# Part of a graph network's gathers loaded row by row through SyncE's queue, with two one-bank PSUM tiles and two input buffers

## The chip, the cores and the metric

The kernel runs on one core of a Trainium2 chip. The metric is the device time of one execution in microseconds (us). Five engines work side by side, each from a queue of its own: TensorE (PE in the profile), VectorE (DVE), ScalarE (ACT), GpSimd (POOL) and SyncE (SP). An engine takes its queue in order: an instruction that waits holds up everything behind it on that engine. SP computes nothing; its queue issues DMA transfers. POOL issues the gathers.

## The reference

Two layers of message passing over one graph of 6250 nodes and 200000 edges, sorted by destination. Every node has 160 float32 features: 64 scalars and 32 vectors of three components. Layer 0 takes 10 inputs per edge for its edge network, layer 1 takes 64; each ends with a residual sum and a layer norm.

```python
def layer(x, src, dst, edge_attr, edge_inputs):        # both layers, cut to what matters
    h = mix(x)                                         # per node, a matrix for scalars, one for vectors
    w = silu(edge_inputs @ W1) @ W2                    # per edge: 192 (layer 0) or 224 (layer 1) weights
    g = h[src]                                         # gather: one row of 160 per edge
    m = products(w, g, edge_attr)                      # per edge: scalar and vector messages
    agg = segment_sum(m, dst, num_segments=6250)       # sum over the edges of a node
    return layernorm(x + node_network(x, agg))
```

The whole computation is float32.

## The kernel before

**Tiles and units.** The edges are cut into 1563 tiles of 128 edges, one edge to a partition; four tiles make a unit, so a layer has 391 units (`windows`, L565). The mixed features `h` of all nodes lie in HBM as `table[0]` (written in a prologue) and `table[1]` (written during layer 0, once a block of nodes is done). Two tiles make a pair; `g`, the gathered rows of a pair, has 8 buffers, thus four units' worth.

**One iteration of the unit loop** (L793 and on), for `u` from -4: the gathers of unit `u + 4` (`gather`, four indirect DMAs, each of 128 rows of 640 bytes, on POOL, L681); the second product of the edge network for unit `u + 2` (`weights`, PE into the PSUM tiles `pw`); the first product for unit `u + 3` (`hidden`, PE into `pair`, then Silu on ACT, L643 and L654); the placement matrices (`places`, DVE, L712) and the messages (`products`, DVE, L699) for unit `u + 2`; and the sum of unit `u` over destination windows (`aggregate`, PE into `pg`). A window that ends is turned and added to the node sums `sm` and `sr` (`turn`, L759 and L761, its place read by a register load on DVE, L756). Between these stand the steps of finished node blocks (`prepare`, `proceed`), which load `nx` (L471 in layer 0, L533 and `no`, L534, in layer 1) through SP.

**Inputs.** The edge network's inputs come in chunks of eight tiles, two units. `inputs` (L603) loads a chunk through SP into one of three buffers, `inputs_of[c % 3]`: two DMAs in layer 0 (L612), four in layer 1 (L620). `hidden` asks for the present chunk and the next. The indices `src` and edge attributes `ea` come for 48 tiles at a time, in two buffers (L589, L590), through SP as well.

**PSUM.** `pair` is one tile of two banks of 512 floats. `hidden` writes its first 256 columns, of both banks in layer 0 and of bank `u % 2` in layer 1; `turn` writes the last 256 columns of bank `g % 2`.

**Order.** A scheduler orders the instructions of each engine from the program's text and its own estimates; the waits for buffers and data are put in by the same framework. PE's products are kept in the program's order (L137 to L145). DMAs of SP take eight semaphores in turn, and one waits until the DMA eight before it has landed.

A check of the destinations (L303) chooses between the path above and a general one; these inputs take the path above.

Of the kernel before, what the change touches and what calls it, by code (L numbers as in the profile page):

```python
# [9 lines left out]
F32 = mybir.dt.float32  # L10
# [17 lines left out]
EC = 8  # L28
BG = 4
ZERO = 8  # L30
ROWS = P * NB + P
EPS = 1e-5
C_S = math.sin(math.pi / 8.0)
# [53 lines left out]
def kernel(ctx: ExitStack, tc: tile.TileContext, a, out):  # L87
# [25 lines left out]
    dram = ctx.enter_context(tc.tile_pool(name="dram", bufs=1, space=bass.MemoryType.DRAM))  # L113


    pair = psum.tile([P, 2, 512], F32, name="pair", bufs=1)

    tail_n, tail_e = N - (NB - 1) * P, E - (NT - 1) * P
    table = [dram.tile([N, D], F32, name=f"table{i}") for i in range(2)]
# [89 lines left out]
    fc1 = [const.tile([P, 100], F32, name="fc1_0"), const.tile([P, P], F32, name="fc1_1")]  # L209
    for t in fc1:  # L210
        nc.gpsimd.memset(t, 0.0)
    for r in (0, 64):
        nc.gpsimd.dma_start(fc1[0][r:r + 10], a["W_fc1"])

    fc2 = [const.tile([100, 192], F32, name="fc2_0"), const.tile([P, 224], F32, name="fc2_1")]
    for c0, at, n in ((64, 0, 64), (0, 64, 64), (128, 128, 64)):
# [32 lines left out]
    def turn_nodes(bs, x):  # L249

        m, n = len(bs), rows_of(bs[0])
        p = psum.tile([P, 512], F32, name="pw", bufs=3)
        for j in range(m):
            transpose(p[:, j * P:j * P + n], x[:n, j, 0:P], ident[:n, :n])
        last = work.tile([P, BG * V], F32, name="xz")
        nc.vector.tensor_copy(last[:n, :m * V].rearrange("p (j d) -> p j d", d=V), x[:n, 0:m, P:D])
        z = pair[:, 0, 0:P]
        transpose(z[:m * V, :n], last[:n, :m * V], ident[:n, :n])
        xt = work.tile([P, BG * P], F32, name="xt", bufs=2)
        zt = work.tile([P, P], F32, name="zt", bufs=2)  # L260
        w = (m - 1) * P + n
        if (bs[0] // BG) % 2:
            nc.scalar.activation(xt[:, :w], p[:, :w], AF.Copy)
        else:
            nc.vector.tensor_copy(xt[:, :w], p[:, :w])
        nc.scalar.activation(zt[:m * V, :n], z[:m * V, :n], AF.Copy)
        return xt, zt

    def send_nodes(bs, xt, zt):
        n = rows_of(bs[0])  # L270
        rows = work.tile([P, BG, D], F32, name="rg", bufs=2)
        qs = []
        for j in range(len(bs)):
            tag, k = (("pg", 2), ("pn", 1), ("pg", 2), (None, 0))[j]
            p = psum.tile([P, 512], F32, name=tag, bufs=k) if tag else pair[:, 1]
# [51 lines left out]
        nc.vector.tensor_reduce(tops[:, 1:2], limits, AX.XY, OP.max)  # L327

    def checked():
        p = pair[:, 0]  # L330
# [66 lines left out]
    for k in range(2):  # L397
        nc.vector.tensor_copy(
            rr0[k * V:k * V + V, :, k * V:k * V + V],
            p[k * V:k * V + V, 192:256].rearrange("p (j d) -> p j d", j=2))  # L400

    nc.sync.dma_start(fc1[1][:64, :64], a["fc_w1"])
    nc.sync.dma_start(fc1[1][64:, 64:], a["fc_w1"])
    for r in (0, 64):
# [157 lines left out]
        return [fetch], [summed]  # L562


    def windows(i, loads, work, inputs_of):  # L565
        nw = (192, 224)[i]


# [34 lines left out]
        def inputs(c):  # L603

            e0 = c * EC * P
            n = min(EC * P, E - e0)
            k, of_e = ((10, a["e10"]), (64, a["e64"]))[i]
            e = inputs_of[c % 3]

            for h in range(2):  # L610
                if i == 0 and n == EC * P:
                    nc.sync.dma_start(  # L612
                        e[h * 64:h * 64 + k].rearrange("p (u m) -> p u m", m=2 * P),
                        of_e[:, e0:e0 + n].rearrange("p (u h m) -> p u h m", h=2, m=2 * P)[:, :, h])
                    continue
                for u in range(0, n, 4 * P):
                    r = u + h * 2 * P
                    m = min(2 * P, n - r)
                    if m > 0:
                        nc.sync.dma_start(e[h * 64:h * 64 + k, u // 2:u // 2 + m],  # L620
                                          of_e[:, e0 + r:e0 + r + m])
            made["e", c] = e

        def hidden(u):

            t0 = 4 * u
            c = t0 // EC
            for k in (c, c + 1):
                if ("e", k) not in made and k * EC < NT:
                    inputs(k)  # L630
            e = made["e", c]
            n = min(4 * P, E - t0 * P)
            h = work.tile([P, 512], F32, name="h", bufs=2)
            at = (t0 % EC) * P // 2
            m = min(n, 2 * P)
            if i == 0:

                halves = [(0, m)] + [(1, n - m)] * (n > m)
                for j, m in halves:
                    k = slice(64 * j, 64 * j + 64)  # L640
                    matmul(pair[:100, j, :m], fc1[0][k], e[k, at:at + m], start=True, stop=True)
                for j, m in halves:
                    nc.scalar.activation(h[:100, 2 * P * j:2 * P * j + m], pair[:100, j, :m], AF.Silu)  # L643
            else:
                p = pair[:, u % 2]
                k = P if n > 2 * P else 64
                if n == 4 * P or n <= 2 * P:
                    parts = ((k, 0, m),)
                else:
                    parts = ((P, 0, n - 2 * P), (64, n - 2 * P, 2 * P))  # L650
                for kk, c0, c1 in parts:
                    matmul(p[:kk, c0:c1], fc1[1][:kk, :kk], e[:kk, at + c0:at + c1],
                           start=True, stop=True)
                    nc.scalar.activation(h[:kk, c0:c1], p[:kk, c0:c1], AF.Silu, scale=0.125)  # L654
            made["h", u] = h

        def weights(ps):
# [5 lines left out]
            for p, j in [(p, j) for p in ps for j in range(2)] if i == 0 else \  # L663
                    [(p, j) for j in range(2) for p in ps]:
                t = 2 * p + j
                if t < NT:
# [5 lines left out]
                        l, r = h[k, j * P:j * P + n], fc2[1][k]  # L672
                    matmul(made["w", p][:n, j, :nw], l, r, start=True, stop=True)

        def gather(p):
            g = work.tile([P, 2, D], F32, name="g", bufs=8)
            for j in range(2):
                t = 2 * p + j
                if t < NT:
                    n = edges_of(t)  # L680
                    nc.gpsimd.indirect_dma_start(  # L681
                        out=g[:n, j, :], out_offset=None, in_=table[i][:, :],
                        in_offset=bass.IndirectOffsetOnAxis(ap=of(t)[0], axis=0))
            made["g", p] = g
# [60 lines left out]

        def turn(g):
            r = made["r", g]
            pt = pair[:, g % 2, 2 * P:]
            if i == 0:
                transpose(pt[:96, :P], r[:, :96], ident)  # L750
                transpose(pt[:64, P:P + W], r[:32, 96:160], ident[:32, :32])
            else:
                transpose(pt[:, :P], r[:, :P], ident)
                matmul(pt[:, P:P + W], rest[g % 3], fold, start=True, stop=True)
            with tc.issue_after(made["last"].ins):
                b = nc.vector.value_load(base[0:1, g:g + 1], min_val=0, max_val=NP - W)  # L756
# [36 lines left out]
        for u in range(-4, units + 1):  # L793
# [3 lines left out]
            if u + 4 < units:  # L797
                for p in pairs_of(u + 4):
                    gather(p)
            if 0 <= u + 2 < units:  # L800
                weights(pairs_of(u + 2))
            if 0 <= u + 3 < units:
# [136 lines left out]
    with tc.If(ok > 0) as cmp:  # L939
        with tc.tile_pool(name="loads", bufs=2) as loads, \  # L940
                tc.tile_pool(name="edges", bufs=2) as work:

            inputs_of = [loads.tile([P, EC * P // 2], F32, name=f"e{k}", bufs=1) for k in range(3)]
            for e in inputs_of:
                nc.vector.memset(e, 0.0)
            for i in range(2):
                windows(i, loads, work, inputs_of)
    with cmp.Else():
        pinned[0] = False
        for i in range(2):  # L950
# [53 lines left out]
```

## Time and profile before

| | us |
|---|---|
| median of 3 runs | 4153.65 (4151.93 to 4154.42) |
| the profiled execution's own time | 4153.7 |
| its span, first to last instruction | 4151.9 |
| busy PE / DVE / POOL / ACT | 3476.9 / 3103.4 / 3018.9 / 1151.1 |
| gathers on POOL (L681) | 3126, 2997.0 busy |

Lines of the profile name a source line (L681 is line 681 of the kernel before), the engine, the operation, and output and input tiles. A group's line ends with its busy time, the mean duration of one in ns, and the idle time of the engine ahead of it, with what ended most of that. "issue" is idle time for which the profile shows no wait. A line of waits has the waiting engine and tile, what released it, the us in total, how often, and the longest. SPq and DVEq are the queues of SP and DVE, where DMA issues, register loads (TENSOR_LOAD), register operations (FUSED_REGOPS) and semaphore instructions are seen; they are not counted as busy. Lines of a source line's instructions give the durations as minimum/median/maximum in ns.

### The profile page before, as it was taken

Reading aid. Unit: us, or ns where it says so; the run is one execution under the profiler, and the core shown is the slowest. Engines: PE = TensorE matmul, PEld = TensorE weight load, DVE = VectorE, ACT = ScalarE, POOL = GpSimd, SP = SyncE. Lnnn points to the kernel's source line nnn. Section 1 sums busy time; section 2 is a strip of 40 time slices with the busy share of each in tenths; the row PEclk is TensorE's granted clock in tenths of the full one; section 3 lists DMA queues with packets and bytes.
Section 4 is the critical chain, followed back from the end, with each engine's and each line's share of the span. In section 5 each row is a group of like instructions: output and inputs, shape, how many; then the busy total and the mean of one; then the engine's idle time right before and its main releaser. Section 6 shows DMA issues by size and latency. Waiting matters only on the chain.

```text
span 4151.9 us, 108120 instructions
## 1 busy us (share of the span) xinstructions
PE 3476.9 (84%) x37265; PEld 2397.6 (58%) x37265; DVE 3103.4 (75%) x13202; ACT 1151.1 (28%) x3915; POOL 3018.9 (73%) x3233
## 2 busy tenths in 40 slices
PE   6888888888999999999977888788787778778887
PEld 4655666566666666666655555455555555555555
DVE  5776666677777777777757777778878888888887
ACT  2111112222223333333321111112223333334444
POOL 3777777777777777776637777777777777777774
PEclk8888889999989999999978888888889999999988
DMA  3222222222233333332223333333333333433332
GB/s 118 72 72 73 76 76 78 79 79 80 79 83 81 83 86 86 85 84 78 76 67 95 95 96 99 98 93 105 100 99 101 105 102 99 108 104 104 104 103 59
DMA packets 305442, 369.59 MB, mean 89 GB/s; under 512 B 87103, under 2 KB 253128, under 8 KB 304888
## 3 DMA queue, kind: packets, MB, share of 16 engines
q0 software_dynamic: 151088, 257.36, 23.6%
q1 hardware_dynamic: 125176, 88.36, 7.5%
q10 hardware_dynamic: 28624, 16.88, 1.3%
q8 instruction: 299, 4.90, 0.5%
q14 instruction: 255, 2.09, 0.2%
HBM read 341.50 MB, written 20.80 MB: 87 GB/s over the span
## 4 chain that ended last, share of the span: by engine, by line
PE 29%; issue 21%; DMA 16%; POOL 15%; DVE 15%; ACT 2%; DVEq 1%; SPq 0%; ACTq 0%; POOLq 0%
DMA g<-table,src 16%; POOL g L681 15%; DVE mid L699 9%; PE pw L138 8%; PE pn L138 7%; PE pg L138 7%; PE pair L138 4%; DVE sel L712 2%; PE pair L143 2%; DVE sm L759 1%; DVEq L756 1%; PE pn L143 1%; ACT L458 1%; DVE sr L761 0%; DVE nx L460 0%
## 5 line engine op out<-in xcount | busy, mean ns | idle before, releaser
L681 POOL DMA_INDIRECT g<-table,src x3126 | 2997.0, 959 | 1088.9 <-issue 722.5
L699 DVE TENSOR_TENSOR mid<-g,pw 128x128 f32<-128x128 f32 (+2 forms) x7820 | 1857.1, 302 | 679.5 <-DMA g<-table,src 463.2
L138 PE MATMUL pw<-fc,h 100*128 100x192 f32 (+1 forms) x6252 | 1188.2, 383 | 133.9 <-DVE mid L699 126.0
L138 PE MATMUL pg<-mid,sel 128*32 128x160 f32 (+1 forms) x25008 | 1170.5, 311 | 0.0
L138 PEld LDWEIGHTS pw<-fc,h 100*128 100x128 f32 (+1 forms) x6252 | 870.2, 203 | 301.3 <-issue 233.6
L138 PEld LDWEIGHTS pg<-mid,sel 128*32 128x32 f32 x25008 | 782.4, 119 | 400.6 <-issue 320.0
L712 DVE SCALAR_TENSOR_TENSOR sel<-iota,off,ea 128x128 f32<-128x128 f32 x3126 | 948.1, 345 | 49.8 <-PE pg L138 35.0
L138 PE MATMUL pair<-e,fc 64*100 64x256 f32 (+1 forms) x2348 | 612.2, 467 | 301.3 <-DVE sr L761 288.1
L138 PEld LDWEIGHTS pair<-e,fc 64*100 64x100 f32 (+1 forms) x2348 | 242.4, 188 | 533.7 <-DVE sr L761 369.9
L643 ACT ACTIVATE h<-pair 100x256 f32<-100x256 f32 x782 | 257.6, 381 | 1018.9 <-PE pair L138 980.3
L654 ACT ACTIVATE h<-pair 128x256 f32<-128x256 f32 x392 | 150.5, 384 | 1021.4 <-PE pair L138 1018.7
L143 PE MATMUL pair<-ident,r 128*96 128x128 f32 (+1 forms) x852 | 227.5, 290 | 104.7 <-DVE sr L761 49.7
L143 PEld LDWEIGHTS pair<-ident,r 128*96 128x96 f32 (+1 forms) x852 | 105.5, 124 | 288.5 <-issue 99.1
L759 DVE TENSOR_TENSOR sm<-pair,sm 96x128 f32 (+1 forms) x568 | 163.2, 287 | 90.8 <-PE pair L143 33.2
L737 ACT ACTIVATE r<-pg 128x96 f32<-128x96 f32 (+1 forms) x568 | 149.9, 264 | 292.6 <-PE pg L138 219.8
L743 ACT ACTIVATE rest<-pg 32x32 f32<-32x32 f32 x1136 | 209.6, 184 | 12.5
L138 PE MATMUL pn<-rm,sm 96*128 96x128 f32 (+4 forms) x980 | 179.5, 339 | 26.7 <-DVE sm L759 25.4
L138 PEld LDWEIGHTS pn<-rm,sm 96*128 96x128 f32 (+3 forms) x980 | 164.9, 222 | 35.6 <-DVE sm L759 29.1
L458 ACT ACT_TABLE_LOAD x97 | 124.5, 1283 | 8.6 <-DVE mv L457 7.0
L138 PE MATMUL pn<-rr,sr 64*128 64x128 f32 (+2 forms) x196 | 62.0, 403 | 53.5 <-DVE sr L761 51.6
L138 PEld LDWEIGHTS pair<-fold,rest 128*128 128x128 f32 x568 | 106.4, 229 | 0.0
L761 DVE TENSOR_TENSOR sr<-pair,sr 64x32 f32 (+1 forms) x568 | 101.6, 179 | 0.8 <-DVE sm L759 0.6
(134 smaller groups left out, 1228.9 us busy)
## 6 DMA issues: line engine op xcount, KB each, us to landing
g<-table,src POOLq DMA_INDIRECT x3126
e<-in_e SPq DMA_DIRECT2D x781, 64.0 KB
e<-in_e SPq DMA_DIRECT2D x390, 20.0 KB
ea<-in_ea_main SPq DMA_DIRECT2D x63, 96.0 KB
xself<-no ACTq DMA_DIRECT2D x48, 96.0 KB
no<-xself SPq DMA_DIRECT2D x48, 96.0 KB
xg<-in_x_main SPq DMA_DIRECT2D x12, 320.0 KB
table<-rg SPq DMA_DIRECT2D x12, 320.0 KB
```

What stands on the lines that cost most here:

```text
L138: r = nc.tensor.matmul(*args, **kw)
L143: r = nc.tensor.transpose(*args)
L458: nc.scalar.activation(mv[:n, 1:2], mv[:n, 1:2], AF.Sqrt, bias=eps[:n])
L643: nc.scalar.activation(h[:100, 2 * P * j:2 * P * j + m], pair[:100, j, :m], AF.Silu)
L654: nc.scalar.activation(h[:kk, c0:c1], p[:kk, c0:c1], AF.Silu, scale=0.125)
L681: nc.gpsimd.indirect_dma_start(out=g[:n, j, :], out_offset=None, in_=table[i][:, :], in_offset=bass.IndirectOffsetOnAxis(ap=of(t)[0], axis=0))
L699: nc.vector.tensor_tensor(parts(mid[:n, :m], V * place, V * step, k), parts(g[:n, :m], c, V, k), parts(q[:n, :m], w, w_step, k), OP.mult)
L712: made["last"] = nc.vector.scalar_tensor_tensor(s[:n, j], iota[:n, None, :].to_broadcast([n, 4, W]), w, e[:, :, None].to_broadcast([n, 4, ...
L737: nc.scalar.activation(r[:, :w], pg[:, :w], AF.Copy)
L743: nc.scalar.activation(rest[g % 3][k, k], pg[k, P:P + V], AF.Copy)
L759: nc.vector.tensor_tensor(sm[:h, :, at], pt[:h, :P].rearrange("p (c w) -> p c w", c=4), sm[:h, :, at], OP.add)
L761: made["last"] = nc.vector.tensor_tensor(sr[:k, at], pt[:k, P:P + W], sr[:k, at], OP.add)
```

## The change

- Four units of each layer, 80, 160, 240 and 320, are no longer gathered by POOL. Their rows, 512 a unit, are loaded one by one through SP, some 1.6 partitions (6.4 rows) in each iteration of the unit loop, into one buffer `gs`. For a partition, SP loads the four sources of its edges from SBUF into registers, and issues four DMAs of one row whose address comes from a register. They are kept in the program's order on SP. The next unit's rows begin in the iteration after the one that multiplies the last unit's rows.
- `row_src` holds the sources of these units, loaded by four DMAs before layer 0.
- `inputs_of` has two buffers in place of three.
- `pair` becomes two tiles of one bank each; nothing else is done with them.
- One of the two loads of `W_fc1` goes from POOL's queue to SP's, further down in the prologue.

```diff
+ROW_UNITS = range(80, (NT + 3) // 4 - 1, 80)
...
-    pair = psum.tile([P, 2, 512], F32, name="pair", bufs=1)
+    pair = [psum.tile([P, 512], F32, name=f"pair{k}", bufs=1) for k in range(2)]
...
-    for r in (0, 64):
-        nc.gpsimd.dma_start(fc1[0][r:r + 10], a["W_fc1"])
+    nc.gpsimd.dma_start(fc1[0][0:10], a["W_fc1"])
...
+    nc.sync.dma_start(fc1[0][64:74], a["W_fc1"])
...
-            e = inputs_of[c % 3]
+            e = inputs_of[c % 2]
...
-                    matmul(pair[:100, j, :m], fc1[0][k], e[k, at:at + m], start=True, stop=True)
+                    matmul(pair[j][:100, :m], fc1[0][k], e[k, at:at + m], start=True, stop=True)
...
-                p = pair[:, u % 2]
+                p = pair[u % 2]
...
+        def in_order(r):
+            tc.keep_in_program_order(r)
+
+        def rows_of_unit(u):
+
+            k = next((k for k, x in enumerate(ROW_UNITS) if x - 4 >= u), None)
+            if k is None:
+                return
+            x = ROW_UNITS[k]
+            begin = (ROW_UNITS[k - 1] - 1) if k else -4
+            if u < begin:
+                return
+            if u == begin:
+                made["rows", x] = work.tile([P, 4, D], F32, name="gs", bufs=1)
+            g, steps = made["rows", x], x - 4 - begin
+            k0, k1 = ((v * P + steps - 1) // steps for v in (u - begin, u - begin + 1))
+            for p in range(k0, min(k1, P)):
+                loads_, v = nc.values_load_multi_w_load_instructions(
+                    row_src[p:p + 1, k, :], engines=[ET.SP], min_val=0, max_val=N - 1,
+                    skip_runtime_bounds_check_because="an edge's source is a node")
+                for r in loads_:
+                    in_order(r)
+                for j in range(4):
+                    in_order(nc.sync.dma_start(g[p:p + 1, j, :], table[i][bass.ds(v[j], 1), :]))
+
         def gather(p):
+            if p // 2 in ROW_UNITS:
+                made["g", p] = made["rows", p // 2][:, 2 * (p % 2):2 * (p % 2) + 2, :]
+                return
...
-            pt = pair[:, g % 2, 2 * P:]
+            pt = pair[g % 2][:, 2 * P:]
...
                 for p in pairs_of(u + 4):
                     gather(p)
+            rows_of_unit(u)
             if 0 <= u + 2 < units:
                 weights(pairs_of(u + 2))
...
-            inputs_of = [loads.tile([P, EC * P // 2], F32, name=f"e{k}", bufs=1) for k in range(3)]
+            inputs_of = [loads.tile([P, EC * P // 2], F32, name=f"e{k}", bufs=1) for k in range(2)]
             for e in inputs_of:
                 nc.vector.memset(e, 0.0)
+            row_src = loads.tile([P, len(ROW_UNITS), 4], I32, name="row_src", bufs=1)
+            for k, u in enumerate(ROW_UNITS):
+                nc.sync.dma_start(row_src[:, k, :], a["src_main"][:, 4 * u:4 * u + 4, 0])
```

More of the change, by code (lines that the diff above doesn't have):

```diff
@@ L256, in turn_nodes @@
         nc.vector.tensor_copy(last[:n, :m * V].rearrange("p (j d) -> p j d", d=V), x[:n, 0:m, P:D])
-        z = pair[:, 0, 0:P]
+        z = pair[0][:, 0:P]
         transpose(z[:m * V, :n], last[:n, :m * V], ident[:n, :n])
@@ L274, in send_nodes @@
             tag, k = (("pg", 2), ("pn", 1), ("pg", 2), (None, 0))[j]
-            p = psum.tile([P, 512], F32, name=tag, bufs=k) if tag else pair[:, 1]
+            p = psum.tile([P, 512], F32, name=tag, bufs=k) if tag else pair[1]
             q = p[:n, :2 * D].rearrange("p (w d) -> p w d", w=2)
@@ L329, in checked @@
     def checked():
-        p = pair[:, 0]
+        p = pair[0]
         transpose(p[:1, :P], over, ident)
@@ L562, in last_nodes, with windows @@
         return [fetch], [summed]
-    def windows(i, loads, work, inputs_of):
+    def windows(i, loads, work, inputs_of, row_src):
         nw = (192, 224)[i]
@@ L640, in hidden @@
                     k = slice(64 * j, 64 * j + 64)
-                    matmul(pair[:100, j, :m], fc1[0][k], e[k, at:at + m], start=True, stop=True)
+                    matmul(pair[j][:100, :m], fc1[0][k], e[k, at:at + m], start=True, stop=True)
                 for j, m in halves:
-                    nc.scalar.activation(h[:100, 2 * P * j:2 * P * j + m], pair[:100, j, :m], AF.Silu)
+                    nc.scalar.activation(h[:100, 2 * P * j:2 * P * j + m], pair[j][:100, :m], AF.Silu)
             else:
-                p = pair[:, u % 2]
+                p = pair[u % 2]
                 k = P if n > 2 * P else 64
@@ L941 @@
                 tc.tile_pool(name="edges", bufs=2) as work:
-            inputs_of = [loads.tile([P, EC * P // 2], F32, name=f"e{k}", bufs=1) for k in range(3)]
+            inputs_of = [loads.tile([P, EC * P // 2], F32, name=f"e{k}", bufs=1) for k in range(2)]
             for e in inputs_of:
                 nc.vector.memset(e, 0.0)
+            row_src = loads.tile([P, len(ROW_UNITS), 4], I32, name="row_src", bufs=1)
+            for k, u in enumerate(ROW_UNITS):
+                nc.sync.dma_start(row_src[:, k, :], a["src_main"][:, 4 * u:4 * u + 4, 0])
             for i in range(2):
-                windows(i, loads, work, inputs_of)
+                windows(i, loads, work, inputs_of, row_src)
     with cmp.Else():
```

## The prediction

> **What bounds the kernel now.** I read the page first. It gives GpSimd (POOL) 73% of the span and TensorE (PE) 84%, so the busy shares don't name the bound. The group of the gathers, L681, does: 1088.9 us of idle time stand before them, and 722.5 us of it waited for nothing.
>
> ```profile
> span 4151.9 us, 108120 instructions
> PE 3476.9 (84%) x37265; PEld 2397.6 (58%) x37265; DVE 3103.4 (75%) x13202; ACT 1151.1 (28%) x3915; POOL 3018.9 (73%) x3233
> ...
> L681 POOL DMA_INDIRECT g<-table,src x3126 | 2997.0, 959 | 1088.9 <-issue 722.5
> ```
>
> Second, the timeline of POOL alone. The gathers stand back to back, 0.95 us each and 0.30 us of issue between them, 1.255 us from start to start.
>
> ```profile
> 1001.21 0.95 POOL L681 DMA_INDIRECT g<-table,src  x1 [0.30 <-issue]
> 1002.47 0.95 POOL L681 DMA_INDIRECT g<-table,src  x1 [0.30 <-issue]
> 1003.72 0.95 POOL L681 DMA_INDIRECT g<-table,src  x1 [0.30 <-issue]
> ```
>
> Third, busy time by stretch (the fifth pair of numbers is POOL's time and count): 317 gathers in 400 us of the first layer and 318 in the second, so a unit of four gathers takes 400/317 x 4 = 5.05 us and 5.03 us. VectorE (DVE) is busy for 268 and 332 of the 400 us. Both layers run at the pace of POOL.
>
> ```profile
> 480.00:880.00 400.00, 339.65 (x3670) 239.65 (x3661) 268.16 (x1066) 85.98 (x268) 303.63 (x317) 0.89 0.29 77
> 3320.00:3720.00 400.00, 311.61 (x3637) 217.72 (x3637) 331.58 (x1517) 140.79 (x512) 303.39 (x318) 0.92 0.38 103
> ```
>
> Fourth, POOL's waits. Only the third column's long ones are true stalls: 52.2 us until the first table stands, 51.2 us between the layers, and some of the 147.9 us for a free `g` buffer.
>
> ```profile
> POOL g L681 <- issue: 722.5, 2370, 0.3
> POOL g L681 <- DVE mid L699: 147.9, 377, 4.1
> POOL g L681 <- DMA g<-table,src: 52.4, 172, 0.3
> POOL g L681 <- DVE rr L398: 52.2, 1, 52.2
> POOL g L681 <- DMA e<-in_e: 51.5, 2, 51.2
> ```
>
> Last, SyncE's queue (SP), on which the change puts its work. It waits for most of the run, because it is ahead: for free input buffers, and for gathers that still use a `src` tile. That is room, and the question is whether it is enough.
>
> ```profile
> SPq L612 <- PE pair L138: 1178.6, 157, 15.2
> SPq L589 <- DMA g<-table,src: 878.7, 160, 25.8
> SPq L620 <- PE pair L138: 712.0, 237, 13.1
> ```
>
> **Removed from POOL.** Four units a layer (80, 160, 240, 320), four gathers each: 32 gathers x 1.255 us = 40 us, 20 us a layer. The later consumers have slack to take it (DVE 67% and 83% busy). So if all else stays hidden, 4153.7 - 40 = 4114 us. 4153.7 us is the profiled execution's own time, 1.8 us over its span and 0.05 us over the median of the runs, 4153.65; sums are made on it.
>
> **Added to SP.** For each of the 128 partitions of such a unit: one load of four registers, four register operations (row number to address), four DMAs of 640 bytes. That is 1024 loads, 4096 register operations and 4096 DMAs, in a queue that holds some 1,500 DMAs now. None of this form is in the trace of before; the nearest rows are these (ns, minimum/median/maximum):
>
> ```profile
> L756 DVEq TENSOR_LOAD <-base x568: 296/303/478, 111.2 to 4139.1; - x190
> L756 DVEq FUSED_REGOPS  x568: 190/190/206, 111.6 to 4139.5; - x190
> L938 SPq TENSOR_LOAD <-flag x1: 476/476/476, 75.8 to 75.8; - x1
> L938 SPq FUSED_REGOPS  x1: 186/186/186, 76.3 to 76.3; - x1
> L471 SPq DMA_DIRECT2D nx<-in_x_main x48: 351/352/461, 77.9 to 2003.6; - x48
> L471 SPq DMA_DIRECT2D nx<-in_x_tail x1: 251/251/251, 2035.7 to 2035.7; - x1
> L612 SPq DMA_DIRECT2D e<-in_e x390: 282/283/1256, 79.4 to 2057.4; - x195
> L620 SPq DMA_DIRECT2D e<-in_e x784: 314/556/1843, 2063.4 to 4091.3; - x196
> ```
>
> Between two instructions of a queue the trace leaves some 0.045 us, 0.08 us after a register load.
> - The register operation: 0.19 us (both rows).
> - The row's DMA: between 0.25 us (the tail of `nx`, the cheapest load of SP) and 0.47 us (the loads of a 64-row tail, L592). I take 0.27 us, near the short ones, since a row is small.
> - The load of four registers: a load of one takes 0.30 us. The Trainium skill speaks against this row: "Runtime: NRT & Kernel Launch", section Instruction fetch mechanics, has about 200 ns for each register even in bulk (for loads from HBM), which would be an estimated 0.80 us; "DMA: Bandwidth & Descriptors", section Latency and other measured facts, has a floor of about 600 ns for a load, spread over four by unrolling. I take 0.60 us. No run here shows four at once.
>
> A partition, four rows, is then 0.60 + 0.08 + 4 x (0.19 + 0.04 + 0.27 + 0.045) = 0.68 + 2.18 = 2.86 us. Ends: 0.38 + 4 x 0.525 = 2.48 us, and, with 0.90 us and 0.35 us, 0.98 + 4 x 0.625 = 3.48 us.
>
> SP's other work over 320 units, the stretch in which rows are loaded (from the start to unit 320; the last 71 units have none). First layer: 320 input DMAs x (0.283 + 0.045) = 105 us, 300 semaphore instructions for them x 0.062 = 19 us, 40 loads of `nx` and theirs 18 us, 27 pairs of `src` and `ea` with theirs 30 us: 172 us. Second: 640 x (0.556 + 0.045) = 385 us, 19 us, 40 pairs of `nx` and `no` 43 us, 27 us: 474 us.
>
> The sums, 512 partitions a layer x 2.86 = 1464 us:
> - first layer 1464 + 172 = 1636 us, against 320 x 5.05 = 1615 us of POOL: 21 us late;
> - second layer 1464 + 474 = 1938 us, against 320 x 5.03 = 1608 us: 330 us late.
>
> **SP becomes the bound, in the second layer clearly.** Its stream is in order: behind every row stand the next input loads and the loads of `src`. In the built program the row DMAs are pinned, and `src` 3, which stood after 28 input DMAs, now stands after 38 of them and 58 partitions. When SP is late, the edge networks (L641) lack their inputs and POOL its indices, so all engines run at SP's pace. POOL's 40 us become idle time. Sum: 4153.7 + 21 + 330 = 4505 us.
>
> The second rule that I weigh stands for the change: "DMA: Bandwidth & Descriptors", section Issuing engines are not separate DMA queues, says that issuing from several engines saves only the time to initiate, usually small beside the transfer. By it the rows would cost nothing seen, and the sum is 4114 us. The rows differ: POOL issues 128 rows in 1.255 us, SP needs at least 4 x 0.525 us for four. Here the time to initiate is the matter. What the rule is about is no concern: the DMA engines are 29% to 38% busy, and 40 us of gathers move over to them as the same bytes.
>
> **The rest.** Two input buffers for three: an input chunk (two units) may now be loaded when the chunk before the current one has been read, three units or 15 us ahead of use, not 25 us. By the trace's semaphore events an input load lands 2.4 us (median, second layer) after its issue, so this costs nothing while SP is on time; if SP is late its cover is gone, and it is in the sum already. A row DMA waits for the one eight DMAs earlier: 8 x 0.55 = 4.4 us, over those 2.4 us. Rows of the next unit wait until DVE has multiplied the last (one `gs` buffer): up to a unit, 5 us, four times a layer, inside the 15 us. In the first layer one half of the first chunk is queued behind four partitions, 11 us; POOL fills 16 buffers in 20 us meanwhile. In the second layer the first rows wait, like the gathers, for the second table; four input loads stand before them. The split of `pair`: PE's order is the same, instruction for instruction, and its waits on `pair` are for reads of the same bank, so nothing, or a few us either way. One load of `W_fc1` goes from POOL to SP: POOL's 52.2 us wait covers it.
>
> **Rivals.**
> 1. Partitions cost 2.5 to 3.0 us each, SP bounds the second layer and touches the first (above): 4505 us; 2.48 us gives 1270 us a layer, the first layer 20 us faster, the second 136 us late, 4270 us; 3.0 us gives 93 + 402, 4649 us.
> 2. They cost more, and both layers are bound by SP. For: the rule of 200 ns a register, the 0.47 us of small loads. Against: the short loads of L612. At 3.48 us, 1782 us a layer: 339 + 648 us late, 5141 us. With the rule's 0.80 us alone, 3.06 us: 124 + 433, 4711 us.
> 3. The other side: SP stays hidden and POOL's time is gained, 4114 us. It is decided in the second layer, by the point where 512 partitions fit into 1608 - 474 = 1134 us, 2.21 us each. For: SP waits some 3000 us now. Against: even with the lowest ends one takes 2.48 us.
> 4. No difference: SP is hidden, but DVE and PE, 83% and 92% busy late in the layers, take over the gain: 4150 us.
>
> **How the numbers follow.** Rival 1 has 0.50, rival 2 0.38, rival 3 0.08, rival 4 0.04. Faster by over 0.2% (what this kernel's times can tell from no change) 0.08, within 0.04, slower 0.88. The prediction is rival 1's 4505 us. The range takes in its low end with 30 us to spare, and rival 2 up to 3.48 us a partition: 4240 to 5150 us. Its own range is 4270 to 4650 us.
>
> **What would show it.** Right: long groups of SP without a wait, up to the two units of 320 and none after; waits of SP for L138 much shorter up to there; waits of PE or ACT for `e`, and of POOL for `src` or `g` buffers, where there were issue gaps; units of about 5.1 us in the first layer and 6 us in the second, 5.05 us after unit 320. The register load of four at 0.6 us, the row's DMA at 0.27 us. Wrong: gathers still 1.255 us apart beside the rows (rival 3), or first-layer units as slow as 5.9 us and more (rival 2). The prediction errs by 1024 us for each us by which a partition is mis-sized, where both layers are bound.

## The result, and the profile after

The changed kernel takes 4213.92 us (median of 4 runs, 4206.46 to 4219.6), the kernel before in the same set 4153.0 us: a ratio of 1.0145, 95% interval 1.0128 to 1.0163. It is slower, as forecast, but by 61 us and not by 351. The profiled execution took 4213.32 us. Some of the experiments below fell into sets of runs in which the kernel before itself takes 6101 to 6207 us, at a lower granted clock of PE (0.74 to 0.77 over a run, against 0.86 to 0.91); why is not known, and every ratio is to the kernel before in the same set, the two kinds of sets being kept apart.

The page of the changed kernel, the lines that answer to those of before (L681 is L710 now, L138 is L139):

```profile
span 4211.5 us, 121593 instructions
PE 3470.8 (82%) x37265; PEld 2404.4 (57%) x37265; DVE 3102.4 (74%) x13201; ACT 1151.4 (27%) x3915; POOL 2987.4 (71%) x3200
...
L710 POOL DMA_INDIRECT g<-table,src x3094 | 2965.7, 959 | 1186.1 <-issue 726.5
...
L139 PE MATMUL pair<-e,fc 64*100 64x256 f32 (+1 forms) x2348 | 620.4, 459 | 456.8 <-DMA e<-in_e 351.0
```

There are 32 gathers fewer, each still 959 ns, and 97 us more idle time in front of those that are left. The last line is the second layer's edge network: its products now wait for their inputs above all, 351.0 us in the whole run. Busy time by stretch:

```profile
480.00:880.00 400.00, 351.68 (x3730) 249.58 (x3728) 272.24 (x1077) 88.56 (x274) 303.31 (x318) 0.88 0.30 79
3320.00:3720.00 400.00, 306.57 (x3422) 209.87 (x3421) 305.37 (x1386) 128.43 (x469) 273.83 (x286) 0.85 0.35 95
```

The first layer's stretch holds 318 gathers, where it held 317; that of the second holds 286 in place of 318, and DVE's time in it falls from 332 to 305 us: all engines run at another's pace. What a row costs SP, from the instructions of the lines that load and issue rows (ns, minimum/median/maximum):

```profile
L693 SPq TENSOR_LOAD <-row_src x1024: 459/563/1711, 68.7 to 3822.1; - x171
```

```profile
L699 SPq FUSED_REGOPS  x4096: 37/37/48, 69.2 to 3824.0; - x196
L699 SPq MOVE gs<-table x4096: 29/29/38, 69.4 to 3824.1; - x196
L699 SPq DMA_DIRECT2D gs<-table x4096: 224/228/316, 69.5 to 3824.1; - x196
```

A partition is one load of 0.563 us and four times 0.037 + 0.029 + 0.228 us, 1.74 us, with 0.56 us of gaps between these: 2.30 us (median from one load's start to the next instruction after the fourth DMA).

SP's waits, longest groups first. The three longest of before, for the same reasons, were 1178.6 (the first line here), 878.7 (the second) and 712.0 us (the fifth): SP is not ahead any more where rows are loaded. The fourth line is new: row DMAs that wait for a store of `xmid` which ScalarE issues.

```profile
SPq L613 <- PE pair L139: 254.0, 70, 13.7
SPq L590 <- DMA g<-table,src: 150.1, 29, 17.5
SPq L621 <- PE pg L139: 118.0, 78, 5.3
SPq L699 <- DMA xmid<-nx: 109.2, 22, 16.9
SPq L621 <- PE pair L139: 65.2, 59, 12.9
```

POOL's waits. The third line, for indices, was not among the long ones before:

```profile
POOL g L710 <- issue: 726.5, 2380, 0.6
POOL g L710 <- DVE mid L728: 117.0, 325, 4.8
POOL g L710 <- DMA src<-in_src_main: 102.9, 19, 10.6
```

**Where the time went**, by the start times of the gathers in the traces: the difference to the kernel before in each part (us), for the changed kernel and for three experiments that are told below. "Rows" is the part from a layer's first gather to unit 330.

| | before | changed | pair alone | merged inputs | half the rows, merged |
|---|---|---|---|---|---|
| start to first gather | 78.8 | -11.1 | -12.7 | -11.4 | -13.3 |
| layer 0, rows | 1670.0 | +6.1 | +3.8 | +8.3 | -12.7 |
| layer 0, rest | 335.7 | -15.4 | -24.0 | -16.9 | -15.8 |
| between the layers | 52.2 | -1.8 | -4.5 | -5.1 | -5.2 |
| layer 1, rows | 1661.6 | +94.7 | -2.2 | +19.5 | -10.5 |
| layer 1, rest | 313.3 | -6.6 | -7.6 | -3.9 | -4.6 |
| last gather to end | 40.3 | -6.3 | -5.9 | -1.9 | -2.0 |
| sum | 4151.9 | +59.6 | -53.1 | -11.2 | -64.1 |

The loss is in the second layer's rows. Something gives 41 us back before, between and after these parts, and the first layer's 20 us of saved gathers are not there.

### The profile page after: what moved, and what is told of

It reads as the page before. It is cut to its first block, busy times and chain, and to the rows that moved or that the text cites. A ratio compares the mean times of both kernels' runs of the same rounds, so it can differ in the third digit from the quotient of the medians.

```text
span 4211.5 us, 121593 instructions
## 1 busy us (share of the span) xinstructions
PE 3470.8 (82%) x37265; PEld 2404.4 (57%) x37265; DVE 3102.4 (74%) x13201; ACT 1151.4 (27%) x3915; POOL 2987.4 (71%) x3200
## 5 line engine op out<-in xcount | busy, mean ns | idle before, releaser
L710 POOL DMA_INDIRECT g<-table,src x3094 | 2965.7, 959 | 1186.1 <-issue 726.5
L728 DVE TENSOR_TENSOR mid<-g,pw 128x128 f32<-128x128 f32 (+2 forms) x7740 | 1819.3, 298 | 569.9 <-DMA g<-table,src 306.1
L139 PE MATMUL pw<-fc,h 100*128 100x192 f32 (+1 forms) x6252 | 1165.8, 386 | 72.7 <-DVE mid L728 53.6
L139 PE MATMUL pg<-mid,sel 128*32 128x160 f32 (+1 forms) x25008 | 1173.5, 312 | 0.1
L139 PEld LDWEIGHTS pg<-mid,sel 128*32 128x32 f32 x25008 | 780.0, 119 | 398.7 <-issue 317.2
L139 PE MATMUL pair<-e,fc 64*100 64x256 f32 (+1 forms) x2348 | 620.4, 459 | 456.8 <-DMA e<-in_e 351.0
L139 PEld LDWEIGHTS pw<-fc,h 100*128 100x128 f32 (+1 forms) x6252 | 869.7, 207 | 218.8 <-issue 156.5
L139 PEld LDWEIGHTS pair<-e,fc 64*100 64x100 f32 (+1 forms) x2348 | 247.7, 186 | 692.4 <-issue 413.1
L139 PE MATMUL pn<-rm,sm 96*128 96x128 f32 (+4 forms) x980 | 172.7, 330 | 25.6 <-DVE sm L788 23.8
L139 PEld LDWEIGHTS pn<-rm,sm 96*128 96x128 f32 (+3 forms) x980 | 157.5, 214 | 34.0 <-DVE sm L788 27.4
L139 PEld LDWEIGHTS pair<-fold,rest 128*128 128x128 f32 x568 | 112.0, 243 | 1.1 <-ACT rest L772 1.1
L139 PE MATMUL pn<-rr,sr 64*128 64x128 f32 (+2 forms) x196 | 59.4, 388 | 49.9 <-DVE sr L790 45.6
```

The source lines that it names most:

```text
L139: r = nc.tensor.matmul(*args, **kw)
L710: nc.gpsimd.indirect_dma_start(out=g[:n, j, :], out_offset=None, in_=table[i][:, :], in_offset=bass.IndirectOffsetOnAxis(ap=of(t)[0], axis=0))
L728: nc.vector.tensor_tensor(parts(mid[:n, :m], V * place, V * step, k), parts(g[:n, :m], c, V, k), parts(q[:n, :m], w, w_step, k), OP.mult)
```

## The experiments

### The changed kernel once more

The file of the change, unedited, beside other runs of the kernel before.

> The changed kernel itself, unchanged, on the chip of this call, as the base for the runs made beside a kernel before of 6100 us. Theory (SyncE's queue is full only where GpSimd sets a pace of 5 us a unit): where the kernel before takes 4153 us, ratio 1.0145 again. Where TensorE is slower and a unit takes 7.6 us, SyncE's 5.2 us of work a unit fit, and the ratio is 0.99 to 1.01, if the amount of work alone matters. Rival (order: the index loads stand behind inputs that wait for a buffer): 1.01 to 1.03 there, above the run with early index loads, 1.004.

Measured: 4211.88 against 4144.73 us, 1.0169 [1.0141, 1.0196]. Its parts differ from the first trace's by 6 us at most (+10.2 in the first layer's rows, +100.6 in the second's), so differences of 10 us in the table above are near what a single profile can tell, and those of 20 us and more are taken as real.

### The split of `pair` alone

```diff
--- the kernel before
-    pair = psum.tile([P, 2, 512], F32, name="pair", bufs=1)
+    pair = [psum.tile([P, 512], F32, name=f"pair{k}", bufs=1) for k in range(2)]
...
-            pt = pair[:, g % 2, 2 * P:]
+            pt = pair[g % 2][:, 2 * P:]
```

(and the other uses of `pair`, as in the change; no rows, three input buffers).

> The kernel before with the split of the PSUM pair alone. Theory: the prologue's transposes no longer wait for the other bank, the first gather starts some 11 us earlier, and nothing else moves, because GpSimd sets the pace: 4131 us (4126 to 4136). Rival (the moved load of W_fc1 makes the prologue shorter): first gather at 89 us, 4142 us.

Measured: 4104.26 (4100.63 to 4109.31) against 4147.59 us, 0.9903 [0.9887, 0.9920]. A part that the prediction put at "nothing, or a few us either way" is worth 43 us, and even the expectation of this run, the prologue's 11 us alone, was too small. One of PE's waits before, then two with the split (the one for `pw` was 126.0 us before):

```profile
PE pair L138 <- DVE sr L761: 288.1, 215, 2.8
```

```profile
PE pw L138 <- DVE mid L699: 212.3, 172, 3.6
PE pair L138 <- DVE sr L761: 145.9, 120, 2.5
```

With one tile, a product into one bank of `pair` also waited for DVE's read of the other (L761, `turn`); the split halves those waits. In the middle of the layers, where POOL is the bound, PE only waits elsewhere (`pw`), and the pace stays 5.01 to 5.12 us a unit. The gain is where POOL isn't the bound: 12.7 us in the prologue, where transposes use one bank and products the other, 24.0 us at the end of the first layer, and 18 us in the later parts. The load of `W_fc1` isn't moved in this kernel, so the earlier start is not its doing.

### The rows taken away, the input loads merged, one more load of registers

Three edits of the changed kernel. Without rows (all gathers on POOL again, `row_src` gone, two buffers and the split kept):

```diff
-            rows_of_unit(u)
```

With the second layer's inputs in two DMAs a chunk, as in the first layer, and not four:

```diff
-                if i == 0 and n == EC * P:
+                if n == EC * P:
```

With a second load of the four registers for each partition, whose values nothing uses:

```diff
+                more_, _ = nc.values_load_multi_w_load_instructions(
+                    row_src[p:p + 1, k, :], engines=[ET.SP], ...)
```

> All gathers are back on GpSimd and no row is loaded through SyncE; the split of the PSUM pair, the two input buffers and the moved load of W_fc1 stay. Theory (SyncE's queue is full in the second layer, because of the rows): 4142 us, the time before less the 11 us by which the first gather starts earlier in the changed kernel; 4135 to 4155. Rival (two input buffers are what makes the inputs late): most of the second layer's loss of 94 us stays, 4190 us or more. Rival (the split pair costs or gains something): more than 10 us from 4142.

> The changed kernel, and in the second layer the two input DMAs of one half of a chunk are one DMA over both units, as the first layer has them: the same bytes, buffers and rows, 320 issues fewer in the units 0 to 320. Theory (queue full): 320 x 0.6 us = 192 us of SyncE's 1653 us go, 1461 us fit into the 1616 us that GpSimd takes for these units, and the layer gains its 20 us of gathers in place of losing 94: 4214 - 94 - 20 = 4100 us (4090 to 4130). Rivals (buffers too few, or row DMAs that slow the other transfers): nothing of theirs has changed, 4190 to 4215 us.

> The changed kernel with every register load of a partition's four sources done twice: 1024 loads more, of 0.56 + 0.06 us, and no DMA more. Theory (queue full): the second layer takes all of it, 512 x 0.62 = 317 us; the first layer now has 1178 + 172 + 317 = 1667 us in SyncE's queue against 1616, so 50 to 100 us more there: 4580 to 4650 us. Rivals (buffers, contention of transfers): no transfer and no buffer has changed, 4200 to 4250 us.

These runs fell into sets with the longer time, so the numbers of microseconds above don't apply; ratios, with one or two repeats each in further sets of that kind:

| edit of the changed kernel | ratio to the kernel before | repeats |
|---|---|---|
| no rows | 0.9739 [0.9704, 0.9774] | 0.9721, 0.9712 |
| merged inputs | 1.0234 [1.0198, 1.0269] | 1.0206, 1.0224 |
| second load | 1.0608 [1.0573, 1.0642] | 1.0610 |

The second load is not in the built program, since its registers feed nothing. The trace of that run shows as many loads as the changed kernel has:

```profile
L698 SPq TENSOR_LOAD <-row_src x1024: 2/492/1657, 67.9 to 5863.7; - x171
```

All that is left of it is one semaphore instruction of 17 ns for each partition. SP's order is that of the changed kernel but for one load of `src` and up to six of `nx`. So this run says nothing of the price of a load; it stands in for the changed kernel, which was not itself run in such a set, at about 1.061. That is an assumption: the next experiment shows that a small difference in SP's order can cost much. With it, the rows cost 8.9% there (1.061 over 0.974), and halving the second layer's input DMAs takes 3.5% away. POOL is not the bound there: without rows it waits 1754.3 us for DVE to free its `g` buffers, and a unit takes 6.7 us or more. SP's work of 5.5 us a unit (1767 us for 320 units of the second layer, with the rows) fits into that, so the amount of work alone doesn't explain the 8.9%.

### The stretches

To have several cases in one run: rows of three units a layer, 160, 240 and 320, each loaded over the 77 iterations before it; the second layer's inputs merged only in the stretch of unit 240; and the added loads again, in the first layer one for unit 160 and two for unit 320, in the second one for unit 320.

```diff
-ROW_UNITS = range(80, (NT + 3) // 4 - 1, 80)
+ROW_UNITS = (160, 240, 320)
...
-            begin = (ROW_UNITS[k - 1] - 1) if k else -4
+            begin = x - 81
...
+                for _ in range(((1, 0, 2), (0, 0, 1))[i][k]):
+                    more, _v = nc.values_load_multi_w_load_instructions(...)
...
-                if i == 0 and n == EC * P:
+                if n == EC * P and (i == 0 or 80 <= c < 120):
```

> The changed kernel with no rows for unit 80, and a different queue load in each stretch of 80 units, two input buffers throughout. First layer: no rows; rows with each register load done twice; rows as they are; rows with each register load done three times. Second layer: no rows; rows as they are; rows with merged input loads; rows with each register load done twice. Expected us a unit, where the kernel before has 5.05 and 5.03. Theory (the amount of work in SyncE's queue against GpSimd's pace; 1.66 partitions a unit of 2.30, 2.92 or 3.54 us, beside 0.54 or 1.48 us of other work, 0.9 us with merged loads): first layer 5.05, 5.4, 5.05, 6.4; second layer 5.03, 5.3 to 5.5, 5.03, 6.3 to 6.5; 4330 to 4420 us in all. Rival (two buffers): 5.03 nowhere in the second layer, and no step with the number of register loads. Rival (place of the index loads): the same pace in all three stretches of rows of a layer.

Measured: 4373.78 us (2 runs) against 4141.68, 1.0562 [1.0522, 1.0602]. The total lies in the expected range, and the reason given for it is wrong: here, too, the added loads are absent, 768 loads for 6 x 128 partitions.

```profile
L699 SPq TENSOR_LOAD <-row_src x768: 457/546/805, 466.7 to 3991.8; - x192
```

All stretches thus do the same work for a partition, and still two of them are far slower than in the changed kernel. From the first register load to the last row of one unit, SP's time in instructions and gaps below 0.12 us ("work"), and in longer gaps ("waits"), from the traces (us):

| | span | work | waits |
|---|---|---|---|
| layer 0, unit 320: changed | 394.1 | 335.2 | 58.9 |
| the same, stretches | 524.3 | 340.2 | 184.1 |
| layer 1, unit 320: changed | 432.5 | 412.3 | 20.3 |
| the same, stretches | 470.2 | 412.7 | 57.5 |
| layer 1, unit 240: changed | 423.7 | 405.0 | 18.7 |
| the same, stretches (merged) | 403.6 | 363.5 | 40.0 |

In the second layer the stretch of unit 320 is 37.7 us longer, its waits are 37.2 us longer, and its work is equal. In the first layer it is 130.2 us longer, 125.2 of it waits. A span is work and waits by definition, so this shows one thing: **with equal work in SP's queue, the time can still be far longer**. That SP's waits are the cause, and not a sign of slowness elsewhere, is read from what they wait for. In the stretches' unit 320 of the first layer, SP and then PE and POOL:

```profile
SPq L705 <- DMA xmid<-nx: 139.0, 13, 15.1
SPq L705 <- DMA table<-nr: 25.9, 13, 3.2
```

```profile
PE pn L144 <- DMA nx<-in_x_main: 66.3, 13, 8.0
```

```profile
POOL g L716 <- DVE mid L734: 87.3, 38, 10.6
POOL g L716 <- issue: 71.6, 234, 0.6
POOL g L716 <- DMA src<-in_src_main: 47.1, 4, 18.1
```

A row DMA has no use for `xmid`. By the semaphore events it waits because ScalarE's store of a node block counts on the same one of the eight semaphores, and the store isn't issued yet. One such wait, with rows on SP from 1409.24 us on (the second of them waits), the store on ScalarE, and the load of `nx` behind the rows:

```profile
1409.24 23.30 SPq L705 DMA_DIRECT2D gs<-table  x16
1422.55 0.33 ACTq L519 DMA_DIRECT2D xmid<-nx  x1
1433.48 0.36 SPq L472 DMA_DIRECT2D nx<-in_x_main  x1
```

SP goes on 1.6 to 2.2 us after each store: stores at 1422.5, 1465.2, 1507.4 and 1548.3 us, SP at 1424.1, 1466.9, 1509.1 and 1550.5. Behind the waiting row stands the load of a later block's `nx` (1433.5, 1476.7, 1517.6, 1560.4), and PE, which takes its queue in order, stands still until that has landed (66.3 us in 13 waits). By the order of these times, the next store is late in its turn: the loop closes through SP's queue, once a block, every 42 us. When this stretch begins, 21 blocks' `nx` have been loaded; in the changed kernel, 22. With one block less ahead, the same rows wait three times as long. That the one makes the other is argued, and why the built order came out so was not found.

### The inputs merged, in a set of the shorter time

> As k1, where the kernel before takes 4145 us: theory 4090 to 4130 us, faster than both kernels; rivals 4185 to 4215 us.

Measured: 4145.71 us (10 runs) against 4141.68, 1.0013 [1.0001, 1.0025]. Neither number was met: merging brings some 55 to 65 us, and what is left of the rows still costs what the split gives. The second layer's rows fall from +94.7 to +19.5 us: SP's work in units 0 to 320 falls from 1653 to 1479 us. The first layer, which the edit doesn't touch, stays at +8.3 us, with 331 us of work and 81 us of waits, on average, in each half of its units 170 to 330. SP's load therefore explains most of the second layer's loss and not the first's.

### Half the rows, the inputs merged

```diff
-ROW_UNITS = range(80, (NT + 3) // 4 - 1, 80)
+ROW_UNITS = range(160, (NT + 3) // 4 - 1, 160)
...
-                if i == 0 and n == EC * P:
+                if n == EC * P:
```

> The changed kernel with two row units a layer in place of four (160 and 320, so a row DMA stands half as often in SyncE's queue) and the second layer's input loads merged. Base: the kernel before at 4142 us, the changed kernel with merged inputs at 4146. Theory (in units 160 to 320 the waits of SyncE's queue for ScalarE's stores, added to 85% of work, fill it): the queue has room for them now, so the 5.2 us a unit there become 5.03, and what is gained stays: 11 us in the prologue and 20 us of gathers, 4111 us (4100 to 4122), faster than both kernels. Rival (two input buffers): the pace of 5.15 to 5.25 us stays in units 160 to 320 and the time is 4130 to 4150 us.

Measured: 4099.04 (4089.63 to 4104.41) against 4147.59 us, 0.9891 [0.9874, 0.9908]: the fastest by its median, just below the expected range, and 49 us below the kernel before. SP is ahead again, and no group of rows that wait is among its long ones:

```profile
SPq L613 <- PE pair L139: 934.2, 242, 12.2
SPq L590 <- DMA g<-table,src: 825.5, 141, 22.0
SPq L535 <- DVE nr L554: 188.6, 29, 11.3
```

Between units 90 and 330, the skipped ones included, a unit takes 4.96 to 5.04 us in both layers: the gathers' time is gained when SP isn't late, and two input buffers show no cost then. Against the split alone, the two parts with rows are 24.8 us faster (20 us of gathers are gone), but the ends of the layers give some 14 us back, and by the medians 5 us stay, within the spread of the runs. Nearly all of this version's gain is the split.

### Three buffers, earlier indices, stores elsewhere

Four more, again in sets with the longer time: the changed kernel with a third input buffer (the space from one message tile in six); with the load of the next `src` and `ea` asked for at the fourth unit of the present ones; merged, with the stores of `xmid` issued by POOL; merged, with the third buffer.

```diff
--- three buffers
-            e = inputs_of[c % 2]
+            e = inputs_of[c % 3]
...
-            mid = work.tile([P, 2, 14 * V], F32, name="mid", bufs=6)
+            mid = work.tile([P, 2, 14 * V], F32, name="mid", bufs=5)
--- earlier indices
+            if 4 * (u + 4) % CH == 12 and 4 * (u + 13) < NT:
+                of(4 * (u + 13))
--- stores elsewhere
-            nc.scalar.dma_start(xmid[rows, :], st["x"][:n])
+            nc.gpsimd.dma_start(xmid[rows, :], st["x"][:n])
```

> The changed kernel with three input buffers again; to make room, the message tiles have five buffers in place of six. Theory (queue full): the order of SyncE's queue and its work are the same, and only its 57 us of waits in the second layer's rows can shrink: 4160 to 4214 us. Rival (two buffers make the inputs late): the loss goes, 4100 to 4130 us.

> The changed kernel with the loads of src and ea for the next 48 tiles written nine units earlier in the program, so that they no longer stand just ahead of the gathers that need them; rows, input buffers and SyncE's work are the same. Theory (SyncE's queue is full in the second layer): where the kernel before takes 4153 us, the inputs stay late whatever the place of src, 4185 to 4214 us, and only the first layer gains up to 15 us. Rival (the place of the index loads behind rows and inputs, not the amount of work, makes GpSimd late, 102.9 us of waits for src in the changed kernel): 4110 to 4150 us. Where TensorE is slower than that and bounds the kernel, the queue is not full, and the rival alone would still gain, some 200 to 300 us of the 6200 us that such a chip takes.

> The changed kernel with merged inputs (4146 us beside 4142), and the first layer's stores of xmid, one per block of nodes, issued by GpSimd and not by ScalarE, so that SyncE's row DMAs no longer share a semaphore with a store that ScalarE has yet to issue (106.8 us of such waits in the first layer of the changed kernel, up to 17 us each). Theory (these waits fill SyncE's queue): the waits go, and in the first layer units 170 to 330 take 5.0 us each in place of 5.24 and 5.15, plus GpSimd's own 0.55 + 0.3 us a store, 0.1 us a unit: 5.1; 4140 to 4165 us in all, because GpSimd pays some 40 us for 49 stores. Rival (two buffers): 5.3 us a unit there, 4175 to 4195 us.

> The changed kernel with merged inputs and three input buffers again (message tiles five in place of six). Theory (work and waits fill SyncE's queue, so it never gets two chunks ahead): 4130 to 4150 us, units 170 to 330 still at 5.15 to 5.25 us. Rival (two buffers take the lead that would bridge the waits): 5.0 us a unit there in both layers and 4085 to 4110 us.

| edit of the changed kernel | ratio to the kernel before |
|---|---|
| (about the changed kernel, above) | 1.061 |
| three buffers | 0.9966 [0.9952, 0.9981] |
| earlier indices | 1.0040 [1.0016, 1.0063], again 1.0037 |
| merged, stores on POOL | 1.0164 [1.0096, 1.0231] |
| merged, three buffers | 0.9848 [0.9801, 0.9895] |

The first two each bring the time back to that of the kernel before, within 0.4%. Against the kernel without rows (0.974) the rows still cost 2.3% and 3.1%, in place of 8.9%. Merged inputs and the third buffer together leave 1.1%; as the merged inputs alone stand at 1.0206 to 1.0234, the expected rival, two buffers as the lack, is borne out in these sets. The indices are the plainest case, POOL's waits with late ones (the run of the absent load) and then with early ones:

```profile
POOL g L715 <- DVE mid L733: 1916.7, 434, 21.9
POOL g L715 <- issue: 787.3, 2525, 2.4
POOL g L715 <- DMA src<-in_src_main: 308.1, 19, 27.1
```

```profile
POOL g L710 <- DVE mid L728: 2040.6, 502, 11.6
POOL g L710 <- issue: 767.5, 2472, 1.5
POOL g L710 <- DVE sel L741: 184.6, 84, 8.1
```

The rows are as many, and SP's work is the same; only 50 loads of `src` and those of `ea` beside them stand earlier in the queue, `src` by some 55 rows, 9 units. The wait of 308.1 us is gone from the list, and the ratio falls from the stand-in's 1.061 to 1.004. There, the rows' price was paid through what stands behind them more than through SP's load. Whether that holds in a set of the shorter time, where POOL's waits for `src` sum to 102.9 us in place of 308.1, was not tried, and neither was the third buffer with all of the rows.

Moving the stores settles nothing: 1.0164 can't be told from 1.0206 to 1.0234. The rows wait for another of ScalarE's stores then (182.3 us for `table<-nr`), and POOL itself waits 113.4 us for the data that it is to store.

## Why the prediction was right or wrong

**The bound, right.** Where no rows are loaded, units in the middle of a layer take 5.0 to 5.1 us (the split alone), and with half the rows the time of the skipped gathers appears.

**SP becomes the bound in the second layer, right; its work, right but for one term.** The other work was put at 474 us and measures 460; with the rows' 1193 us it makes 1653 us. The failed term, and the largest of the errors, is the price of a partition, 2.86 us with a low end of 2.48, where 2.30 was measured. In it the register operation is 0.037 us, not 0.19, with a MOVE (a copy of a register) of 0.029 that the sum lacked; the DMA 0.228, not 0.27; the load 0.563, not 0.60. The low end was no bound, because it kept the register operation at the rows of other forms (L756, L938). The price came out 0.09 us above the point of decision, 2.21, so nearly the rival of a hidden SP. With 2.30 us the prediction's own sums are 1178 + 172 = 1350 us for the first layer, hidden, 20 us gained, and 1178 + 474 = 1652 us for the second, 44 us late: 4178 us in place of 4505. This term alone puts the result below the range.

**The rules that were weighed.** A load of four registers took 0.563 us here (median). About 200 ns a register (the Trainium skill, "Runtime: NRT & Kernel Launch", Instruction fetch mechanics), an estimate of 0.80 us for four, didn't hold. The floor of about 600 ns (the Trainium skill, "DMA: Bandwidth & Descriptors", Latency and other measured facts) was the better guide, though no floor here: the shortest of these loads took 0.459 us. That issuing from another engine saves only the usually small time to initiate (the same page, Issuing engines are not separate DMA queues) would have made 4114 us; here four rows with their registers took 2.30 us of SP's time, and that was the price.

**SP's waits, wrong.** The sum took SP's queue as work alone: when late, it never waits. In the second layer, units 0 to 320, it worked 1653 us, as 1652 says (the rows 15 us more, the rest 14 us less), and waited another 57: 1710 us against 1616 before. A unit took 5.3 to 5.5 us there from unit 90 on, not 6. The step is "A row DMA waits for the one eight DMAs earlier: 8 x 0.55 = 4.4 us, over those 2.4 us." It counted only SP's own DMAs; stores of ScalarE count on the same semaphores, and some 35 us of the waits in these rows are for its stores of `out`.

**First layer, wrong in size and in reason.** It was to be 21 us late by SP's work. SP had time, 1354 us of work in 1622, and with 2.30 us it should have gained 20 us; +2.3 us were measured against the split alone. The 22 us between are lost in units 170 to 330 (5.17 and 5.18 us a unit), where the trace shows the rows' waits for stores and PE's for `nx`, as in the stretches. From 880 to 1710 us, SP and then PE:

```profile
SPq L699 <- DMA xmid<-nx: 66.0, 16, 11.0
PE pn L144 <- DMA nx<-in_x_main: 25.2, 14, 6.5
```

In the kernel before PE has no such wait in this stretch. That the time can grow so at equal work is shown in the stretches; that these waits are the 22 us is argued, and the one attempt at them, the stores on POOL, settled nothing.

**The split of `pair`, wrong.** "Its waits on `pair` are for reads of the same bank" was the failed step. Alone the split gives 43 us by the medians, 53 by the profiles.

**Who waits, right.** `e` for PE (351.0 us), `src` for POOL (102.9 us). "This costs nothing while SP is on time", said of the two buffers, held (half the rows); once SP is late the cover is gone, and in the sets of the longer time the third buffer was worth 6% against the stand-in, and 4% with merged inputs.

The terms together, against the kernel before (us, by the profiles): second layer's work +44, SP's waits in it +53, first layer -20 and +22, ends of the layers +13.5 against the split alone, the split -53: +59.5, where +59.6 was measured. This agreement proves nothing, because the +53, the +22 and the ends are what is left over between the traces and the terms before them; the 57 us of waits in SP's queue are the one independent sign. The size fell below the range by two mis-sized terms that point the same way (the partition: 4505 to 4178; the split) and one missing term of the other sign, SP's waits. The sign came right with luck: SP's work alone, rightly priced, makes +24 us, and the split takes 53 away again, so that without the waits, which the sum lacked, the kernel would have come out faster.

## What to carry to other kernels

A queue that takes on small DMAs pays for each instruction and makes everything behind them late: size the price by the exact form of instruction, or bound it from zero where no row of that form exists, and then look at which loads stand behind. Put loads that other engines can't do without (indices, blocks' data) well ahead of the small ones, and see which other engine's DMAs count on the same semaphores. Two banks used by different engines should be two tiles, even where a buffer was cut in halves by index: here this is worth 43 us, where the gathers taken from POOL could give 40.

## What the runs showed of the hardware

- On SP, a load of four registers takes 0.563 us (median); a load of one took 0.476 us there (one instruction) and takes 0.303 us on DVE. A register operation takes 37 ns in this form, where other forms took 186 and 190 ns.
- A DMA of one row with its address from a register takes 0.228 us of SP's time, the cheapest of SP's loads; those of the inputs take 0.283 us in the first layer and 0.556 us in the second (kernel before).
- DMAs of SP and stores of ScalarE count on the same eight semaphores in these programs: rows on SP waited 109.2 us for stores that ScalarE had yet to issue.
- In these programs a product into one bank of a PSUM tile of two banks waited for a read of the other: with a tile for each bank, PE's waits for these reads fall from 288.1 to 145.9 us.
- A load whose registers nothing reads leaves no load in the built program; only the trace tells.
